# A Strassen cross-attention kernel: combinations summed in PSUM banks that are read in between, neighbouring groups of products interleaved, each engine's order written out

## Chip, cores and metric

One NeuronCore of a Trainium2 chip runs the whole program. The metric is the device time of one execution in microseconds (us), as a median of three runs. TensorE is PE in the profile, VectorE DVE, ScalarE ACT, GpSimd POOL; SP issues most DMAs.

## What is computed

For each of 32 batches, with C = 256 channels and N = 1024 positions, all in float32:

```python
x_q = jnp.einsum('oc,bcn->bno', w_qk, y)
x_k = jnp.einsum('oc,bcn->bon', w_qk, x)
x_v = jnp.einsum('oc,bcn->bon', w_v, x) + b_v[None, :, None]
energy = jnp.einsum('bnc,bcm->bnm', x_q, x_k)
attention = jax.nn.softmax(energy, axis=-1)
attention = attention / (1e-07 + attention.sum(axis=1, keepdims=True))
x_r = jnp.einsum('bcn,bnm->bcm', x_v, attention)
x_r = jax.nn.relu(jnp.einsum('oc,bcn->bon', w_t, x - x_r) + b_t[None, :, None])
return x + x_r
```

Here y is `ctx_2048`. The kernel folds the weights: energy is y against (w_qk^T w_qk) x, and w_t is multiplied into w_v once, at the start.

## The kernel before

Each large product of a batch is a 2x2 block product done with seven products instead of eight (Strassen in Winograd's form): products p1 to p7 of block sums, then sums of the products. There are four such groups in a batch:

- `keys` (L240): seven products of 128x512 from the folded weights and the blocks and sums of x (`xs`). They give `gx`, and four POOL sums of its blocks give `gt`.
- `values` (L278): seven products, each as four position tiles of 128 columns, so eight instructions (a float32 matmul is two instructions). They give `ut`, and four POOL sums `us`.
- `energy` (L366): for each of four tiles t, seven products of 128x512. DVE adds two parts into the rows `e` and takes their minimum or maximum in the same instruction (`block`, L384); ACT takes the exponential of the two rows of 1024 (L414); `share` (L427) adds the rows, divided by their sums, into `acc` (L433).
- `attend` (L461): after `columns` (L437) has formed rc, the inverse column sums, through one small product pS (L445), DVE multiplies the rows of e by both scales (`normal`, L471, rows of 1024) and forms four block sums (`less`, L477). Each of the seven products is one x-part (`xpart`, L489) and four tiles of e (`epart`, L494) in one bank. Results go through ACT (bias and Relu), POOL (adds x, L511) and SP (stores).

In `keys`, `values` and `attend` a first product p1 is copied out, p5 is copied out and p6 is summed onto p5's bank; every other product has a bank of its own. PSUM has eight banks, taken in turn by `bank` (L69). `kept` (L208) is the ACT copy out of a bank.

The loop over batches (L552) runs the four energy tiles of batch b, then keys and values of batch b + 1, then `columns` and `attend` of batch b. A scheduler of the tile framework orders the instructions of each engine; `tc.issue_after` pins a few POOL operations and the first product of an energy tile behind others. The sums of x and y blocks are formed by DMA: plain loads on SP's queue and three accumulating DMAs each on POOL's queue (`inputs` L214, `queries` L343, `accumulate` L98), `xsteps` during the energy tiles and `ysteps` after the keys.

Of the kernel before, what the change touches and what calls it, by code (L numbers as in the profile page):

```python
# [9 lines left out]
F32 = mybir.dt.float32  # L10
# [6 lines left out]
def kernel(  # L17
# [56 lines left out]
    def load_x(b, pieces=1):  # L74
        xt = xp.tile([P, KC, N], F32, tag="x", name=f"x_{b}")
        from_ = x[b].rearrange("(k p) n -> p k n", p=P)
        W = KC // pieces
        for j in range(pieces):
            nc.sync.dma_start(xt[:, ts(j, W)], from_[:, ts(j, W)])
        loaded[b] = xt  # L80

    def load_y(b):
        yt = yp.tile([P, KC, N], F32, tag="y", name=f"y_{b}")
        nc.sync.dma_start(yt, y[b].rearrange("(k p) n -> p k n", p=P))
        return yt
# [12 lines left out]
    def accumulate(into, from_):  # L98
        return nc.gpsimd.dma_start(into, from_, accum_op=ALU.add)
# [15 lines left out]
    uc = const.tile([P, 3, P], F32, name="uc")  # L115
    fold = const.tile([P, NG, G32], F32, name="fold")
    nc.sync.dma_start(wqk, w_qk.rearrange("(k p) c -> p k c", p=P))
    load_x(0, KC)
# [4 lines left out]
    yt = load_y(0)  # L123


    zeros = scratch[:, 5, :MB]
# [6 lines left out]
    def lefts(name, ps, sign=1.0):  # L133
# [13 lines left out]
        stt(s1, p21, -1.0, a22, ALU.add)  # L147
        stt(s3, p11, 1.0, a21, ALU.subtract)
        stt(s2, p11, -1.0, s1, ALU.subtract)
        stt(s4, p12, -1.0, s2, ALU.subtract)  # L150
# [26 lines left out]
    def value_bias(wtT):  # L177


        bvb = scratch[:, 6, : KC * P].rearrange("p (k c) -> p k c", k=KC)  # L180
        pb = bank("pb")
        for k in range(KC):
            nc.vector.tensor_copy(bvb[:, k, :], bv[:, k, :].to_broadcast([P, P]))
            nc.tensor.matmul(
                pb[:, :C], bvb[:, k, :], wtT[:, k, :], start=(k == 0), stop=(k == KC - 1)
            )
        nc.scalar.mul(uc[:, 0, :], pb[:, :P], -1.0)
        nc.vector.tensor_tensor(uc[:, 1, :], pb[:, P:C], uc[:, 0, :], ALU.add)
        nc.scalar.mul(uc[:, 2, :], pb[:, P:C], -2.0)
# [12 lines left out]
    def temp(tag, name, pool=cp):  # L202
        return pool.tile([P, MB], F32, tag=tag, name=name)

    def matmul(into, lhs, rhs, onto=False):
        nc.tensor.matmul(into, lhs, rhs, start=not onto, stop=True, skip_group_check=onto)  # L206

    def kept(p, tag, name, pool=cp):  # L208

        s = temp(tag, name, pool)  # L210
        nc.scalar.copy(s, p)  # L211
        return s

    def inputs(b):  # L214

        xs = up.tile([P, 4, MB], F32, tag="xs", name=f"xs_{b}")
        t1, t3, t4, t2 = (xs[:, j] for j in range(4))
        xq = quarters(x[b])
        if b == 0:
            xt = loaded[b]  # L220
            x11, x12 = xt[:, 0, ts(0, MB)], xt[:, 0, ts(1, MB)]
            x21, x22 = xt[:, 1, ts(0, MB)], xt[:, 1, ts(1, MB)]
            add(t1, x11, x12)
            add(t2, x22, t1)
            add(t3, x12, x22)
            add(t4, x21, t2)
            steps = []
        else:
            nc.sync.dma_start(xs[:, :2], xq[:, 0, 1:2, :].to_broadcast([P, 2, MB]))
            nc.sync.dma_start(xs[:, 2:], xq[:, 1])  # L230
            steps = [
                lambda: accumulate(xs[:, :2], corners(x[b])),
                lambda: accumulate(xs[:, 2:], xs[:, 0:1].to_broadcast([P, 2, MB])),
                lambda: accumulate(t4, xq[:, 1, 1]),
            ]
        return (lambda xt: (
            xt[:, 0, ts(0, MB)], xt[:, 1, ts(0, MB)], xt[:, 1, ts(1, MB)], t4, t1, t2, t3
        )), steps

    def keys(b, xr):  # L240

        gx = one.tile([P, KC, N], F32, tag="gx", name=f"gx_{b}")
        g11, g12 = gx[:, 0, ts(0, MB)], gx[:, 0, ts(1, MB)]
        g21, g22 = gx[:, 1, ts(0, MB)], gx[:, 1, ts(1, MB)]

        def gproduct(into, j, onto=False):
            matmul(into, g_left[j - 1], xr[j - 1], onto)

        p1, p2, p3, p4, p56, p7 = (bank(f"pg{j}_{b}") for j in (1, 2, 3, 4, 5, 7))
        gproduct(p1, 1)  # L250
        p1s = kept(p1, "p1s", f"g1s_{b}")
        gproduct(p2, 2)
        gproduct(p56, 5)
        p5s = kept(p56, "p5s", f"g5s_{b}")
        nc.vector.tensor_tensor(g11, p2, p1s, ALU.add)
        gproduct(p3, 3)
        gproduct(p7, 7)
        gproduct(p56, 6, onto=True)
        w = temp("w", f"gw_{b}")
        nc.vector.tensor_tensor(w, p56, p1s, ALU.add)  # L260
        nc.vector.scalar_tensor_tensor(g22, p7, -1.0, w, ALU.mult, ALU.subtract)
        nc.vector.scalar_tensor_tensor(g12, p3, -1.0, w, ALU.mult, ALU.subtract)
        v = temp("v", f"gv_{b}")
        if b == 0:
            nc.vector.tensor_tensor(v, g22, p5s, ALU.add)
        else:
            add(v, g22, p5s)
        gproduct(p4, 4)
        nc.vector.tensor_tensor(g21, p4, v, ALU.subtract)
        gt = one.tile([P, 4, MB], F32, tag="gt", name=f"gt_{b}")  # L270
        t1, t2, t3, t4 = (gt[:, j] for j in range(4))
        sub(t1, g12, g11)
        sub(t3, g22, g12)
        sub(t2, g22, t1)
        last = sub(t4, t2, g21)
        return (g11, g21, g22, t4, t1, t2, t3), last

    def values(b, xr):  # L278

        ut = up.tile([P, NT, C], F32, tag="ut", name=f"ut_{b}")  # L280

        def uproduct(into, j, onto=False):

            for t in range(HT):
                nc.tensor.matmul(  # L285
                    into[:, ts(t, P)],
                    xr[j - 1][:, ts(t, P)],
# [6 lines left out]
        def tiles(p):  # L294
            return p.rearrange("p (t c) -> p t c", t=HT)

        def bias(i):
            return uc[:, i : i + 1, :].to_broadcast([P, HT, P])

        def quadrant(half, i):  # L300
            return ut[:, half * HT : half * HT + HT, ts(i, P)]

        def block(half, i, p, s):
            nc.vector.tensor_tensor(quadrant(half, i), tiles(p), s, ALU.add)  # L304

        def biased(p, i, tag, name):

            s = temp(tag, name)
            nc.vector.tensor_tensor(tiles(s), tiles(p), bias(i), ALU.subtract)
            return s  # L310

        p1, p3, p4, p56, p7 = (bank(f"pu{j}_{b}") for j in (1, 3, 4, 5, 7))
        uproduct(p56, 5)
        p5s = biased(p56, 2, "p5s", f"u5s_{b}")
        uproduct(p1, 1)
        p1s = biased(p1, 0, "p1s", f"u1s_{b}")
        uproduct(p3, 3)
        uproduct(p7, 7)
        uproduct(p4, 4)
        uproduct(p56, 6, onto=True)  # L320
        w = temp("w", f"uw_{b}")
        nc.vector.tensor_tensor(w, p56, p1s, ALU.add)
        w1 = temp("v", f"uw1_{b}")
        add(tiles(w1), tiles(w), bias(1))
        block(1, 0, p3, tiles(w))
        uproduct(p1, 2, onto=True)
        block(0, 0, p1, bias(0))
        block(1, 1, p7, tiles(w1))
        v = temp("v", f"uv_{b}")
        last = sub(tiles(v), quadrant(1, 1), tiles(p5s))  # L330
        block(0, 1, p4, tiles(v))
        us = up.tile([P, 4, HT, P], F32, tag="us", name=f"us_{b}")
        s1, s2, s3, s4 = (us[:, j] for j in range(4))
        a11, a12, a21, a22 = quadrant(0, 0), quadrant(1, 0), quadrant(0, 1), quadrant(1, 1)
        steps = [
            lambda: add(s1, a21, a22),
            lambda: sub(s2, s1, a11),
            lambda: sub(s3, a11, a21),
            lambda: sub(s4, a12, s2),
        ]  # L340
        return (a11, a12, s4, a22, s1, s2, s3), steps, last

    def queries(b, yt):  # L343

        ys = one.tile([P, 4, MB], F32, tag="ys", name=f"ys_{b}")
        s3, s1, s2, s4 = (ys[:, j] for j in range(4))
        y11, y12 = yt[:, 0, ts(0, MB)], yt[:, 1, ts(0, MB)]
        y21, y22 = yt[:, 0, ts(1, MB)], yt[:, 1, ts(1, MB)]
        yq = quarters(y[b])
        if b == 0:  # L350
            add(s1, y21, y22)
            add(s2, s1, y11)
            add(s3, y11, y21)
            add(s4, y12, s2)
            steps = []
        else:
            nc.sync.dma_start(ys[:, :2], yq[:, 0, 1:2, :].to_broadcast([P, 2, MB]))
# [257 lines left out]
```

## Time and profile before

| | |
|---|---|
| median of 3 runs | 2506.15 us (2501.49 to 2508.46) |
| the profiled execution | 2508.91 us, of which its span 2507.0 us |
| TensorE busy | 2284.4 us, 91% of the span, 6366 matmuls |
| VectorE busy | 1821.6 us, 73% |
| ScalarE busy | 607.6 us, 24% |
| GpSimd busy | 1191.8 us, 48% |
| mean granted TensorE clock | 0.957 |

Matmuls are pipelined, so the records of neighbouring ones overlap: what a product costs is read from the distance between starts, not from the mean duration of a record. A stage of the work is read by windows of time, a wait by what ended it, and the chain of work by the timeline of one period.

### The profile page before, as it was taken

Reading aid. Unit: us, or ns where it says so; the run is one execution under the profiler, and the core shown is the slowest. Engines: PE = TensorE matmul, PEld = TensorE weight load, DVE = VectorE, ACT = ScalarE, POOL = GpSimd, SP = SyncE. Lnnn points to the kernel's source line nnn. Section 1 sums busy time; section 2 is a strip of 40 time slices with the busy share of each in tenths; the row PEclk is TensorE's granted clock in tenths of the full one; section 3 lists DMA queues with packets and bytes.
Section 4 is the critical chain, followed back from the end, with each engine's and each line's share of the span. In section 5 each row is a group of like instructions: output and inputs, shape, how many; then the busy total and the mean of one; then the engine's idle time right before and its main releaser. Section 6 shows DMA issues by size and latency. Waiting matters only on the chain.

```text
span 2507.0 us, 20193 instructions
## 1 busy us (share of the span) xinstructions
PE 2284.4 (91%) x6366; PEld 1096.3 (44%) x6366; DVE 1821.6 (73%) x3125; ACT 607.6 (24%) x1033; POOL 1191.8 (48%) x839
## 2 busy tenths in 40 slices
PE   9988899899999999999899988999888999899997
PEld 5444444444444444344444444444444434444442
DVE  6778767787677786777867768677787667876776
ACT  3212232122221222311223212232122321222212
POOL 5444544445544545444454444544445444455442
PEclk9999999999999999999999999999999999999998
DMA  4333443444344344434444333443344334443420
GB/s 134 89 102 88 116 110 88 109 92 110 105 104 99 96 101 113 118 82 101 91 121 110 87 99 88 122 110 88 109 88 112 107 88 109 96 106 105 103 61 17
DMA packets 109739, 249.05 MB, mean 99 GB/s; under 512 B 8640, under 2 KB 9408, under 8 KB 109632
## 3 DMA queue, kind: packets, MB, share of 16 engines
q0 software_dynamic: 42656, 81.28, 19.9%
q1 hardware_dynamic: 66432, 166.48, 19.8%
q8 instruction: 51, 0.84, 0.1%
q14 instruction: 56, 0.46, 0.1%
q10 hardware_dynamic: 544, 0.00, 0.0%
HBM read 181.67 MB, written 33.55 MB: 86 GB/s over the span
## 4 chain that ended last, share of the span: by engine, by line
PE 66%; DVE 16%; POOL 11%; issue 4%; DMA 3%; ACT 1%; POOLq 0%; ACTq 0%; DVEq 0%
PE po L496 32%; PE pe L206 24%; POOL v L64 4%; PE pg L206 4%; PE pu L285 3%; DVE e L473 3%; POOL gt L67 3%; DMA xs<-in_x_dram 3%; PE po L490 2%; DVE ut L304 2%; DVE acc L433 2%; DVE e L388 2%; DVE rc L456 1%; POOL gv L64 1%; POOL uw L64 1%
## 5 line engine op out<-in xcount | busy, mean ns | idle before, releaser
L511 POOL TENSOR_TENSOR ot<-ot,x 128x512 f32<-128x512 f32 x128 | 255.0, 1992 | 543.7 <-ACT ot L510 543.7
L64 POOL TENSOR_TENSOR v<-e,p5s 128x512 f32<-128x512 f32 x128 | 218.7, 1709 | 434.5 <-DVE nm L388 434.5
L206 PE MATMUL pe<-gt,ys 128*128 128x512 f32 x768 | 387.2, 601 | 0.6 <-ACT p5s L211 0.3
L496 PE MATMUL po<-e,ut 128*128 128x512 f32 x512 | 291.1, 707 | 103.9 <-DVE e L473 101.3
L473 DVE SCALAR_TENSOR_TENSOR e<-e,ri,rc 128x1024 f32<-128x1024 f32 x256 | 311.6, 1279 | 1.1
L433 DVE SCALAR_TENSOR_TENSOR acc<-e,ri,acc 128x1024 f32<-128x1024 f32 x224 | 290.9, 1299 | 1.2
L206 PE MATMUL pe<-gx,y 128*128 128x512 f32 x512 | 261.4, 592 | 0.0
L496 PE MATMUL po<-et,us 128*128 128x512 f32 x512 | 231.0, 594 | 1.1
L206 PEld LDWEIGHTS pe<-gt,ys 128*128 128x128 f32 x768 | 140.6, 190 | 205.5 <-issue 145.7
L496 PE MATMUL po<-e,us 128*128 128x512 f32 x512 | 230.2, 592 | 0.0
L496 PEld LDWEIGHTS po<-e,ut 128*128 128x128 f32 x512 | 107.5, 222 | 279.8 <-DVE e L473 193.1
L414 ACT ACTIVATE e<-e,nm 128x1024 f32<-128x1024 f32 x128 | 147.0, 1149 | 255.0 <-DVE nm L388 255.0
L414 ACT ACTIVATE e<-e,bias 128x1024 f32<-128x1024 f32 x128 | 147.0, 1149 | 234.3 <-DVE bias L411 234.3
L388 DVE CUSTOM_DVE_ANT_0 e<-pe,v,nm 128x512 f32<-128x512 f32 x128 | 96.1, 751 | 147.7 <-POOL v L64 147.7
L211 ACT COPY o1s<-po 128x512 f32<-128x512 f32 x32 | 18.8, 586 | 702.2 <-PE po L496 702.2
L496 PEld LDWEIGHTS po<-et,us 128*128 128x128 f32 x512 | 96.5, 190 | 129.3 <-issue 126.2
L496 PEld LDWEIGHTS po<-e,us 128*128 128x128 f32 x512 | 97.3, 190 | 122.5 <-issue 122.5
L480 DVE TENSOR_TENSOR et<-e,et 128x1024 f32<-128x1024 f32 x128 | 150.7, 1219 | 0.0
L206 PEld LDWEIGHTS pe<-gx,y 128*128 128x128 f32 x512 | 97.2, 190 | 122.0 <-issue 99.3
L206 PE MATMUL pe<-gt,y 128*128 128x512 f32 x256 | 130.7, 592 | 0.0
L206 PE MATMUL pe<-gx,ys 128*128 128x512 f32 x256 | 130.7, 592 | 0.0
L388 DVE CUSTOM_DVE_ANT_0 e<-pe,p1s 128x512 f32<-128x512 f32 x128 | 87.0, 680 | 59.6 <-PE pe L206 59.6
(123 smaller groups left out, 3596.1 us busy)
## 6 DMA issues: line engine op xcount, KB each, us to landing
y<-in_ctx_dram SPq DMA_DIRECT2D x32, 1024.0 KB, 8.8
out_dram<-ot SPq DMA_DIRECT2D x128, 256.0 KB, 2.0
x<-in_x_dram SPq DMA_DIRECT2D x31, 1024.0 KB, 5.8
xs<-in_x_dram SPq DMA_DIRECT2D x62, 512.0 KB, 4.2
ys<-in_ctx_dram SPq DMA_DIRECT2D x62, 512.0 KB, 6.7
xs<-in_x_dram POOLq DMA_DIRECT2D x31, 512.0 KB, 6.1
xs<-xs POOLq DMA_DIRECT2D x31, 512.0 KB, 5.0
ys<-in_ctx_dram POOLq DMA_DIRECT2D x31, 512.0 KB, 5.9
```

The costliest lines, as they stand in the source:

```text
L64: return nc.gpsimd.tensor_tensor(out_, in0, in1, ALU.add)
L67: return nc.gpsimd.tensor_tensor(out_, in0, in1, ALU.subtract)
L206: nc.tensor.matmul(into, lhs, rhs, start=not onto, stop=True, skip_group_check=onto)
L285: nc.tensor.matmul(into[:, ts(t, P)], xr[j - 1][:, ts(t, P)], u_left[j - 1], start=(t == 0 and not onto), stop=(t == HT - 1), skip_group_c ...
L304: nc.vector.tensor_tensor(quadrant(half, i), tiles(p), s, ALU.add)
L388: nc.vector.tensor_tensor_reduce(out=e[:, n, ts(h, MB)], in0=in0, in1=in1, scale=1.0, scalar=(BIG if n < HT else -BIG) if first is None el ...
L414: nc.scalar.activation(e[:, n, :], e[:, n, :], AF.Exp, bias=bias[n], scale=-1.0 if n == low else 1.0, accum_out=rs,)
L433: nc.vector.scalar_tensor_tensor(acc, e[:, n, :], scales[n], acc, ALU.mult, ALU.add)
L473: nc.vector.scalar_tensor_tensor(e[:, n, :], e[:, n, :], scales[n], rc, ALU.mult, ALU.mult)
L480: nc.vector.tensor_tensor(out_[:, two], in0[:, two], in1[:, two], ALU.subtract)
L496: last = nc.tensor.matmul(into[:, cols], ur[j - 1][:, t], er[j - 1][:, t, cols], start=False, stop=(t == HT - 1), skip_group_check=True,)
L511: nc.gpsimd.tensor_tensor(ot, ot, xt[:, i, there], ALU.add)
```

## The change

The four groups become subclasses of one class `Seven`. A group now has three banks: `one` takes p1, then p6, p7 and p4 summed onto it; `two` takes p5, then p3; `three` takes p2. Between these, the running sum is read out of the bank: after p1 (p1s), after p5 (p5s), after p6 (w), after p7 (c22), after p4 (c21). Each read is one that the next product onto the bank has to wait for.

- An `InOrder` wrapper fixes the order of instructions on TensorE, VectorE, ScalarE and GpSimd to that of the text. DMAs issued by `nc.sync` are not in it.
- p4 of an energy tile comes in the next tile, behind p6; that of the last tile among the keys; the attention's p4 (`end`) behind p5 of the next batch's first energy tile.
- Keys, values and the end of the energy are interleaved; parts of the values (u.c22, u.p4, u.c21, u.c11, u.c12) lie inside `Attention.run`.
- `normal` works on halves of rows (512 columns). The first share is done by ACT (`acc` = scaled copy).
- The last energy block is the bank itself plus a tile of zeros (DVE); POOL's v sums go. The energy's operands change sides (y's sums are the stationary ones).
- The attention's bias is added by ACT when it copies p1s, p5s and w (Identity with bias); DVE does max(z, 0) + x in one operation. POOL's output add goes.
- The values' bias is added by an accumulating DMA from a broadcast row (`bias`). `us` has one buffer, not two. The loads of x are one batch later in the text.

The diff, cut to its core:

```diff
+    class InOrder:
+        def __getattr__(self, name):
+            def call(*args, **kwargs):
+                behind = nullcontext() if self.last is None else tc.issue_after(self.last.ins)
+                with behind:
+                    self.last = getattr(self.engine, name)(*args, **kwargs)
+                return self.last
...
+    pe, dve, act, pool = (InOrder(g) for g in (nc.tensor, nc.vector, nc.scalar, nc.gpsimd))
...
+        def p1(self):
+            self.one = self.bank(1)
+            self.product(self.one, 1)
+            self.p1s = self.kept(self.one, "p1s")
+
+        def p5(self):
+            self.two = self.bank(5)
+            self.product(self.two, 5)
+            self.p5s = self.kept(self.two, "p5s")
+
+        def p2(self):
+            self.three = self.bank(2)
+            self.product(self.three, 2)
+
+        def p6(self):
+            self.product(self.one, 6, True)
+            self.w = self.kept(self.one, "w")
+
+        def p3(self):
+            self.product(self.two, 3, True)
+
+        def p7(self):
+            self.product(self.one, 7, True)
+
+        def p4(self):
+            self.product(self.one, 4, True)
+
+        def c11(self):
+            self.combine(0, 0, self.three, self.p1s, ALU.add)
+
+        def c12(self):
+            self.combine(0, 1, self.two, self.w, ALU.subtract)
+
+        def c22(self):
+            self.combine(1, 1, self.p5s, self.one, ALU.subtract)
...
+            pool.tensor_tensor(s1, a21, a22, ALU.subtract)
+            pool.tensor_tensor(s2, s1, a11, ALU.subtract)
+            pool.tensor_tensor(s3, a11, a21, ALU.subtract)
+            pool.tensor_tensor(s4, s2, a12, ALU.add)
...
+        def bias(self):
+            accumulate(self.ut, uc.to_broadcast([P, NT, C]))
...
+        def c21(self):
+            self.combine(1, 0, self.one, zeros, ALU.add)
...
+        def biased(self, p, tag, bias):
+            s = temp(tag, f"o{tag}_{self.b}")
+            act.activation(s, p, AF.Identity, bias=bias, scale=1.0)
+            return s
...
+        def run(self, u):
+
+            self.normal(0, 0)
+            if u:
+                u.c22()
+            self.normal(1, 0)
+            self.normal(0, 1)
+            self.mix(self.t1, self.b11, self.b12, ALU.add)
+            self.normal(1, 1)
+            self.mix(self.t2, self.t1, self.b22, ALU.subtract)
+            self.epart(self.one, 1)
+            self.p1s = self.biased(self.one, "p1s", bt[:, 0, :])
+            if u:
+                u.p4()
+                u.c21()
+            self.epart(self.three, 2)
+            self.xpart(self.one, 6, True)
+            self.epart(self.two, 5)
+            self.p5s = self.biased(self.two, "p5s", bt[:, 1, :])
+            self.c11()
+            if u:
+                u.c11()
+                u.c12()
+            self.xpart(self.two, 3, True)
+            self.epart(self.two, 3, range(HT // 2))
+            self.epart(self.one, 6)
+            self.w = self.biased(self.one, "w", nbt[:, 0, :])
+            self.mix(self.t3, self.b12, self.b22, ALU.subtract)
+            self.mix(self.t4, self.b21, self.t2, ALU.subtract)
+            self.epart(self.two, 3, range(HT // 2, HT))
+            self.c12()
+            self.xpart(self.one, 7, True)
+            self.epart(self.one, 7)
+            self.c22()
...
+        for t in range(HT):
+            now = Energy(b, t, lhs, rhs)
+            pair.append(now)
+            now.p1()
+            if t > 0:
+                pair[t - 1].exp(1)
+            now.p5()
+            if t == 0:
+                if before is not None:
+                    before.end()
...
+            if t > 1:
+                pair[t - 2].share(0)
+            now.p2()
+            now.c11()
+            if t == 0 and before is not None:
+                before.c21()
+                if b + 1 < B:
+                    load("x", b + 1)
...
+            now.p6()
+            if t == 1:
+                act.activation(acc, e[:, HT, :], AF.Copy, scale=scales[HT])
+            if t > 0:
+                pair[t - 1].p4()
+                pair[t - 1].c21()
+                pair[t - 1].exp(0)
+            now.p3()
+            now.c12()
+            now.p7()
+            now.c22()
+            usteps[t]()
+            if more and t == 0:
+                xn, xsteps = summed("x", b + 1)
+            elif more:
+                xsteps[t - 1]()
...
+            g = Keys(b + 1, xn)
+            g.p1()
+        last.exp(1)
         if more:
+            g.p5()
+        pair[2].share(0)
+        last.p4()
+        last.c21()
+        last.share(1)
+        if more:
+            load("y", b + 1)
+            rhs, ysteps = summed("y", b + 1)
+            g.p6()
+        last.exp(0)
+        if more:
+            g.p2()
+            g.c11()
+            g.p3()
+        last.share(0)
+        part = columns(b)
+        if more:
+            g.p7()
+            g.c12()
+            g.c22()
+            un = Values(b + 1, xn)
+            un.p1()
+            un.p5()
+            un.p2()
+            un.p6()
+        rc = inverse(b, part)
+        if more:
+            un.p3()
+            g.p4()
+            g.c21()
+            un.p7()
+            lhs = g.factors()
+
+        now = Attention(b, xr, ur)
+        now.begin()
+        if more:
+            ysteps[0]()
+            now.run(un)
+            ysteps[1]()
+            un.bias()
+            ysteps[2]()
```

## Rows read from the trace of the kernel before

**Rows 1.** Windows by stage: length; busy PE, PEld, DVE, ACT, POOL; clock; DMA share; GB/s.

```profile
1185.40:1209.90 24.50, 24.49 (x57) 10.47 (x56) 16.54 (x41) 10.86 (x19) 12.18 (x11) 1.00 0.47 108
1209.90:1221.70 11.80, 7.44 (x15) 2.85 (x14) 10.54 (x24) 4.68 (x8) 5.97 (x5) 0.89 0.67 201
1221.70:1231.10 9.40, 9.40 (x61) 8.91 (x60) 4.85 (x8) 0.00 (x0) 7.51 (x7) 0.77 0.21 32
1231.10:1264.00 32.90, 30.59 (x70) 12.59 (x69) 24.97 (x26) 3.30 (x5) 12.33 (x8) 1.00 0.33 79
```

**Rows 2.** TensorE's waits: line, releaser, us in total, times, longest.

```profile
PE po L496 <- DVE e L473: 101.3, 31, 4.9
PE pg L206 <- DMA xs<-in_x_dram: 46.3, 20, 3.3
PE pg L206 <- ACT g5s L211: 24.0, 31, 0.8
```

**Rows 3.** Timeline of TensorE in the attention: start, us, operation, idle before.

```profile
1245.89 3.60 PE L496 MATMUL po<-e,ut 128*128 128x512 f32 x8
1249.32 3.60 PE L496 MATMUL po<-e,us 128*128 128x512 f32 x8
```

**Rows 4.** Timeline of TensorE in keys and values.

```profile
1215.18 1.13 PE L206 MATMUL pg<-xs,gs 128*128 128x512 f32 x2 [0.78 <-ACT g5s L211]
1219.88 2.05 PE L206 MATMUL pg<-xs,g 128*128 128x512 f32 x2 [3.58 <-DVE gx L261]
...
1228.24 1.06 PE L285 MATMUL pu<-wvtTs,xs 128*128 128x128 f32 x8
1229.13 1.06 PE L285 MATMUL pu<-wvtT,x 128*128 128x128 f32 x8
```

**Rows 5.** Timeline of TensorE: first and last batch's first energy product, pS, last product.

```profile
24.84 1.02 PE L206 MATMUL pe<-gx,y 128*128 128x512 f32 x2
...
2430.35 1.02 PE L206 MATMUL pe<-gx,y 128*128 128x512 f32 x2
...
2465.86 0.63 PE L445 MATMUL pS<-part,fold 128*128 128x32 f32 x2 [10.81 <-DVE ri L454]
...
2495.75 3.60 PE L496 MATMUL po<-et,ut 128*128 128x512 f32 x8
```

**Rows 6.** Groups of instructions by form: shapes, count, busy us, mean ns, idle before.

```profile
L433 DVE SCALAR_TENSOR_TENSOR acc<-e,ri,acc 128x1024 f32<-128x1024 f32 x224 | 290.9, 1299 | 1.2
L414 ACT ACTIVATE e<-e,nm 128x1024 f32<-128x1024 f32 x128 | 147.0, 1149 | 255.0 <-DVE nm L388 255.0
L388 DVE CUSTOM_DVE_ANT_0 e<-pe,v,nm 128x512 f32<-128x512 f32 x128 | 96.1, 751 | 147.7 <-POOL v L64 147.7
L510 ACT ACTIVATE ot<-c,bt 128x512 f32<-128x512 f32 x64 | 46.2, 722 | 337.1 <-DVE c L530 273.9 <-DVE c L534 63.2
L211 ACT COPY g5s<-pg 128x512 f32<-128x512 f32 x32 | 18.8, 587 | 1.1 <-PE pg L206 1.1
```

**Rows 7.** Timeline of VectorE around rc and in the block sums.

```profile
1232.24 0.35 DVE L450 RECIPROCAL sc<-sc 128x32 f32<-128x32 f32 x1
...
1234.10 1.24 DVE L456 STREAM_TRANSPOSE rc<-sc 128x1024 f32<-128x1024 f32 x1
...
1251.76 2.35 DVE L480 TENSOR_TENSOR et<-e,et 128x1024 f32<-128x1024 f32 x2
```

**Rows 8.** Timeline of GpSimd at the end of the attention.

```profile
1250.29 4.94 POOL L511 TENSOR_TENSOR ot<-ot,x 128x512 f32<-128x512 f32 x1 [10.66 <-ACT ot L510]
...
1261.52 1.27 POOL L67 TENSOR_TENSOR ov<-c,o5s 128x512 f32<-128x512 f32 x1 [0.69 <-DVE c L534]
```

**Rows 9.** DMA issues: destination and source, queue, count, KB each, median us to landing.

```profile
xs<-in_x_dram POOLq DMA_DIRECT2D x31, 512.0 KB, 6.1
xs<-xs POOLq DMA_DIRECT2D x31, 512.0 KB, 5.0
...
xs<-in_x_dram POOLq DMA_DIRECT2D x31, 256.0 KB, 8.5
```

More of the change, by code (lines that the diff above doesn't have):

```diff
@@ L200, with temp @@
     sp = ctx.enter_context(tc.tile_pool(name="sp", bufs=4))
-    def temp(tag, name, pool=cp):
-        return pool.tile([P, MB], F32, tag=tag, name=name)
+    def temp(tag, name):
+        return cp.tile([P, MB], F32, tag=tag, name=name)
     def matmul(into, lhs, rhs, onto=False):
[L206 to L218, printed above, removed]
-        if b == 0:
[L220 to L226, printed above, removed]
+        pe.matmul(into, lhs, rhs, start=not onto, stop=True, skip_group_check=onto)
@@ L236, in inputs @@
[L236 to L276, printed above, removed]
@@ L292, in uproduct, with tiles @@
                 )
-        def tiles(p):
+        def tiles(self, p):
             return p.rearrange("p (t c) -> p t c", t=HT)
[L297 to L357, printed above, removed]
-            nc.sync.dma_start(ys[:, 2:], yq[:, :, 0])
+        def block(self, i, h):
+            return self.ut[:, h * HT : h * HT + HT, ts(i, P)]
@@ L359, in queries @@
             steps = [
[L360 to L391 removed]
+                lambda: pool.tensor_tensor(s1, a21, a22, ALU.add),
@@ L478, in less @@
             for j in range(HT // 2):
                 two = ts(j, 2)
[L480 to L499 removed]
+                dve.tensor_tensor(out_[:, two], in0[:, two], in1[:, two], op)
@@ L500, in epart, with xpart @@
+        def xpart(self, into, j, onto=False):
+            pe.matmul(
+                into, t_left[j - 1], self.xr[j - 1], start=not onto, stop=False, skip_group_check=True
+            )
+        def epart(self, into, j, tiles=range(HT)):
+            for t in tiles:
+                pe.matmul(
+                    into,
+                    self.ur[j - 1][:, t],
+                    self.er[j - 1][:, t],
                     start=False,
@@ L552 @@
+    u.c12()
+    u.p7()
+    u.c22()
+    u.p4()
+    u.c21()
+    u.bias()
+    before = None
     for b in range(B):
         more = b + 1 < B
-        e = ep.tile([P, NT, N], F32, tag="e", name=f"e_{b}")
-        acc = one.tile([P, N], F32, tag="acc", name=f"acc_{b}")
-        if more:
-            sums, xsteps = inputs(b + 1)
-        for t in range(HT):
-            with tc.issue_after(last.ins) if (t == 0 and b > 0) else nullcontext():
-                behind = energy(b, t, lhs, rhs, e)
-            for step in usteps[t : t + 1] + (xsteps[t : t + 1] if more else []):
-                with tc.issue_after(behind.ins):
-                    behind = step()
-            if t > 0:
-                share(e, acc, t - 1)
@@ L567 @@
-        share(e, acc, HT - 1)
-        if more:
-            xn = sums(loaded[b + 1])
-            yt = load_y(b + 1)
-            lhs, ysteps = queries(b + 1, yt)
-            rhs, behind = keys(b + 1, xn)
-            with tc.issue_after(behind.ins):
-                ysteps[0]()
-            un, usteps, behind = values(b + 1, xn)
-            for step in ysteps[1:]:
-                with tc.issue_after(behind.ins):
-                    behind = step()
-        rc = columns(b, acc)
-        last = attend(b, xr, ur, e, rc)
@@ new lines @@
+        if more:
+            g.p7()
+            g.c12()
+            g.c22()
+            un = Values(b + 1, xn)
[6 more added lines that the diff above has]
+            un.p3()
+            g.p4()
+            g.c21()
+            un.p7()
+            lhs = g.factors()
+        now = Attention(b, xr, ur)
[6 more added lines that the diff above has]
+            ysteps[2]()
+            before = now
+            xr, u = xn, un
+        else:
+            now.run(None)
+            now.end()
+            now.c21()
```

390 lines of the change are left out of this document (203 added, 187 removed).

## The prediction

> **What bounds the kernel now.** I read the stages first. One period, from the first energy product of a batch to that of the next, is 78.6 us in the slice shown, and TensorE (PE) is busy in nearly all of the energy stage but in only 7.44 of the 11.8 us of the keys stage; no other engine is near its limit, for VectorE (DVE) sums to 56.9 us over the four stages [rows 1]. The list of TensorE's waits says which wait ends last: normalised attention rows (101.3 us), x sums that arrive late by DMA (46.3 us), and a ScalarE (ACT) copy of a product that must be read before the next product may go onto its bank, 31 times 0.8 us [rows 2].
>
> The unit of the sum is one product of two 128x512 instructions. Eight instructions begin at 1245.89 and the next eight at 1249.32, so a product takes 3.43/4 = 0.858 us [rows 3]. A values product (eight instructions of 128 columns) takes 1229.13 - 1228.24 = 0.89 us [rows 4]. A batch has 28 energy, 7 key and 35 attention products (7 x-parts, 7 of four tiles) and 7 value products: 70 x 0.858 + 7 x 0.89 = 66.3, with pS (two instructions of 32 columns, at most two of the eight above, so under 0.22; I take 0.2) **66.5 us**. Thirty-one periods lie between 24.84 and 2430.35 [rows 5]: 77.6 us each. So 11.1 us of a period are waits or half clock, and that is all the change can win, since it removes no product. In the slice: keys 11.8 against 7 x 0.858 = 6.0; values with one x-part 9.4 against 7.3; attention with the other 34 products 32.9 against 29.2; energy 24.5 against 24.0. The loss in the values is clock: the granted clock there is 0.77, with gaps of 0.78 and 3.58 us ahead of it in the keys [rows 1, 4].
>
> **The change, part by part.** *Products interleaved.* Keys now wait between their own products. In the new order g.p6, p2, p3, p7 (3.43 us) and un.p1, p5, p2, p6 (3.57) run while DVE and ACT finish the last energy tile; pS, un.p3, g.p4, un.p7 and three x-parts (0.2 + 0.89 + 0.86 + 0.89 + 2.57 = 5.4) run while DVE forms rc. So epart(1) can start 12.4 us after the end of the last energy p4 (time 0). DVE, at their durations [rows 6, 7]: c21 to 0.75, share(1) to 2.05; exp(0) on ACT starts after g.p6 and its copy (0.86 + 0.59) and ends at 2.6; g.c11 meanwhile, share(0) with its reciprocal to about 4.1; columns (taken as the transpose of the same shape, 1.24) 5.4, so pS at 7.0 has its input; g.c12, g.c22 to 6.9; after pS two small operations of at most 0.35 and the transpose, 7.2 + 0.7 + 1.24 = 9.1. Normalising is cut into halves of 512 columns: half of share's 1.30, 0.65 each (no such form is shown; below, 0.61 by the pitch that back-to-back operations would keep; above, 0.75 of the energy block; I take 0.65, the same operation at half the columns). The first tile is ready at 9.75, 2.6 us ahead of its use; before, four whole rows stood ahead of the first e-part. The 101.3 us go, and what is late next is checked along the same chain: t1's first half is ready at 9.1 + 12 x 0.65 + 0.75 + 1.2 = 18.9 (a pair of such sums takes 2.35 [rows 7]), and epart(5) needs it at 12.4 + 3.43 + 0.89 + 3.43 + 0.86 = 21.0. t3, at about 30, is needed at 34. The least slack is 2.1 us.
>
> *Banks used twice.* Each group of seven now has three banks and four hand-offs, where a product waits until ACT or DVE has read the bank; TensorE's later products are queued behind each. One uncovered hand-off to ACT is the row with 0.78 us of idle [rows 4] (a copy of 0.587 [rows 6] and 0.2 of signals); to DVE it is 0.75 + 0.2 = 0.95. Cover: p1 to p6, two products (1.7 us); p6 to p7, one or more (0.86 at least); p7 to p4, two products where it is least; p5 to p3, two or three. One has none: in the attention xpart 3 follows epart(5) at once. Its reader is an Identity with bias, which is not shown: between the copy's 0.587 and the biased Relu's 0.722; I take the second, as it also adds a bias. So + 0.9 us a period. Within an energy tile, ACT does p1's copy, exp of the tile before, p5's copy: 0.9 + 0.6, to 2.75, to 3.4, and p3 is due at 4.3. If that cover is gone, each tile pays up to 0.8.
>
> *DVE's and POOL's work.* Off DVE: four w sums of energy, two operations in keys and four in values (10 x about 0.7) and the first share, now ACT's; on it: three more in the attention. That is some 6 us less of 56.9, so about 51 in the new period: not the bound, but an exact order makes each lateness queue. GpSimd (POOL) loses the output add and the energy v sum; this work was mostly hidden, and I count no gain for it beyond the chain above. ACT gains seven w copies, two c21 copies and the acc scaling (9 x 0.59 + 1.15), loses three Relus (2.2): some 4 us in an engine that is mostly idle.
>
> *DMA.* New: the bias of the values as an accumulating transfer of 1 MB a batch in POOL's queue, behind ysteps[1] and ahead of ysteps[2] and of the next batch's usteps and xsteps. Price: xs<-xs moves 512 KB in 5.0 us [rows 9]; twice the bytes give 10, four times the pieces (1 KB each, not 2) give 20. I take 12, nearer to the bytes. Issued at about 34, it lands at 46; the first us sum then runs at 47 to 50, before the x loads are in, and nothing on the path waits. At 20 it delays the x sums (rival 2). The xs loads may start only when the last x-part of the attention before has read the tile, which now lies in the next energy stage (about 40; 46 if SP keeps the order of the text behind the x load). With 6 us to load, then 7, 6 and 7 us for three accumulations [rows 9], t2 is there at 59 to 65 and needed at 67.
>
> **The sum.** Period: 66.5 + 0.9 + 0.4 for waits that I can't place (the energy stage already loses 24.5 - 24.0) = **67.8 us**. Before the first energy product: 24.84 now, plus one uncovered DVE hand-off (u.p4 on u.p7's bank), 25.7. Last batch: nothing covers it. 63 products x 0.858 = 54.1; p4 behind c22 0.95; from p4 to pS c21, two shares with exp(0) and columns, 5.0 (10.81 idle before [rows 5]); pS 0.2; three x-parts at half clock + 2.6; p5s 0.9; xpart 4 behind c22 0.95; and a tail, now 2507.0 - 2495.75 - 3.43 = 7.8 [rows 5], without POOL's add 6.5. Together 71.2. Total 25.7 + 31 x 67.8 + 71.2 = 2198.7 us of span, + 1.9 (the profiled run's 2508.9 against its span of 2507.0) = 2200.6; the profiled run lies 2.8 above the median of 2506.15, so I forecast **2200**. At the floor of 66.5 a period it is 2160.
>
> **Rivals.** *1, POOL starved.* An output add issued at 1250.29 took 4.94 us where another took 1.27, and ended 1.1 us after the back-to-back DVE sums that end at 1254.11: POOL waited for DVE's whole run [rows 7, 8]. The new order puts g.factors (four POOL adds) where DVE normalises and sums with hardly a pause from 9 to 32 us, and ysteps[0] is queued behind them. s1 to s3 can start at 6.9, when DVE works on PSUM and small tiles; only s4 needs g.c21 (9.6). If the adds first get through when DVE rests at about 33, ysteps[0] lands at 34 + 6.1 = 40 and p5 of the next energy, due at 38.2, waits 2 to 3 us: 70.5 a period, **2284**. Against it: DVE's reads of banks between 24 and 27 leave room. The Trainium skill, SBUF — State Buffer, Who interferes with whom, says that a DVE instruction with two SBUF inputs keeps out a GpSimd instruction that reads SBUF; the trace agrees by its 4.94 us, and by that rule this rival holds wherever no one-input operation falls in between.
>
> *2, x sums late.* With the bias at 20 us, usteps end at 57 and t2 comes at 57 + 7 + 6 = 70, 3 us late: 70.8, **2293**. For it: 46.3 us of this wait already [rows 2], and a transfer's landing of up to 8.5 us for 256 KB [rows 9]. That SP's queue is not among the orders fixed by hand belongs here: the change then does only part of what it says.
>
> *3, clock.* If a gap of about a microsecond a period lowered the clock, the products behind it would run at half rate as in the values stage now (2.1 us lost, and part of the keys): + 2.7, **2284**. Against it: after the 0.78 us gap the pair of products took 1.13 us, and the attention stage shows a granted clock of 1.00 [rows 1, 4]. The Trainium skill, TensorE: Matmul & The Clock Gate, A second HAM failure mode, reports a kernel whose cycling through PSUM banks idled TensorE often enough to make its clock fall again and again; no run here shows that yet.
>
> *4, slower.* Hand-offs uncovered in general: each order is fixed, so if ACT or DVE lags TensorE by one product, all 28 hand-offs of a period stop it. 28 x 0.78 = 21.8 us make 88.3 a period and **2830**; more than 14 of the 28 uncovered (11 / 0.78) decide for slower. Against it: covers of 0.86 to 4 us at all but one.
>
> **Chances.** Forecast (2160 to 2240) 0.60; rival 1 0.10; rival 2 0.12; rival 3 0.06; a few hand-offs uncovered (2310 to 2490) 0.05; equal 0.03; rival 4 0.04. The range from the floor to a period of 71.3, 2162 to 2310, holds the forecast and rivals 1 to 3. Faster than by 0.3% (about what a measurement of this kernel can tell from no change) 0.93, within it 0.03, slower 0.04.
>
> **What would show it.** Right: periods of 67 to 69 us, a granted clock near 1.00 in every stage, TensorE's waits led by xpart 3 behind ACT with 0.9 us each, none on normalised rows. Wrong: a wait of TensorE on ys (rival 1) or xs (rival 2), a clock below 0.95 without long gaps (3), or waits on ACT copies and DVE combinations spread over energy tiles (4). The forecast fails most easily at the DMA chains, where the trace before shows least.

## The result and the profile after

The changed kernel takes **2219.47 us** (2216.27 to 2220.56), 0.886 of the kernel before (95% interval 0.8841 to 0.8884); 2200 was forecast, in a range of 2162 to 2310. Its profiled execution took 2216.27 us with a span of 2214.5 us. Line numbers no longer tell operations apart, since all go through the wrapper at L77; the names of the tiles do (`op5s` is the attention's copy of p5, `et` its block sums t1, t2, t4, `ep1s` and `ew` the energy's copies).

The page's line of busy time, share of the span and instructions:

```profile
PE 2166.1 (98%) x6366; PEld 1054.7 (48%) x6366; DVE 1772.2 (80%) x2963; ACT 785.2 (35%) x1321; POOL 617.5 (28%) x488
```

TensorE's waits (us in total, times, longest), the three longest:

```profile
PE po L77 <- ACT op5s L77: 26.8, 32, 0.8
PE po L77 <- DVE et L77: 5.4, 21, 0.3
PE pS L77 <- DVE part L77: 5.3, 1, 5.3
```

Windows of one period: keys with the last energy p4; values with pS, g.p4 and three x-parts; attention; the next energy tiles with the attention's p4.

```profile
core 0: us, PE busy (x) PEld busy (x) DVE busy (x) ACT busy (x) POOL busy (x), PEclk, DMA share, GB/s
1004.59:1010.85 6.26, 6.26 (x16) 2.58 (x14) 5.97 (x16) 5.14 (x9) 0.00 (x0) 1.00 0.90 283
1010.85:1019.87 9.02, 9.02 (x60) 7.11 (x59) 8.61 (x10) 2.35 (x4) 5.21 (x4) 1.00 0.10 38
1019.87:1045.56 25.69, 24.57 (x64) 10.99 (x63) 23.29 (x29) 2.65 (x4) 5.54 (x5) 1.00 0.51 85
1045.56:1073.78 28.22, 27.82 (x66) 11.93 (x65) 18.31 (x40) 14.21 (x24) 8.45 (x7) 1.00 0.69 165
```

The same 6366 matmuls run; the granted clock is 1.00 in all four stages, where the values had 0.77 [rows 1]. All three waits of [rows 2] are gone: rows and xs are in no wait of TensorE any more, and g5s is covered. The first window's seven products (six of the keys and the last energy p4) take 6.26 us, where the seven of the keys took 11.8 before; pure product time is 6.0. What is left stands in the attention, 25.69 us for six e-parts of four tiles, three x-parts and u.p4, 27 x 0.858 + 0.89 = 24.1. (The energy window is 0.8 us above its 32 products, most of it a ScalarE copy, ep1s, that came late here and one other time in the run.) The timeline shows where the attention's time goes:

```profile
1019.87 3.60 PE L77 MATMUL po<-e,ut 128*128 128x512 f32 x8
1023.30 1.05 PE L77 MATMUL pu<-wvtT,xs 128*128 128x128 f32 x8
1024.19 3.60 PE L77 MATMUL po<-e,ut 128*128 128x512 f32 x8
1027.63 1.02 PE L77 MATMUL po<-xs,wtTs 128*128 128x512 f32 x2
1028.93 3.67 PE L77 MATMUL po<-et,us 128*128 128x512 f32 x8 [0.28 <-DVE et L77]
1033.44 1.12 PE L77 MATMUL po<-x,wtTs 128*128 128x512 f32 x2 [0.84 <-ACT op5s L77]
1034.40 1.88 PE L77 MATMUL po<-e,us 128*128 128x512 f32 x4
```

epart(5) begins 1028.93 - 1027.63 - 0.86 = 0.44 us late; xpart 3 begins 1033.44 - 1028.93 - 3.43 = 1.08 us late, of which 0.84 is recorded as idle, and the next product comes another 0.10 late (0.96 for 0.86). A short gap costs some 0.2 to 0.3 us beyond the idle that the record shows: 0.16 because a product's record (1.02 us) outlasts the distance between starts (0.86), and about 0.1 because the product behind the gap takes longer.

Why t1 is late: VectorE's timeline in the same period,

```profile
1016.66 5.09 DVE L77 SCALAR_TENSOR_TENSOR e<-e,ri,rc 128x512 f32<-128x512 f32 x4
1021.67 0.67 DVE L77 TENSOR_TENSOR ut<-up5s,pu 128x512 f32<-128x512 f32 x1
1022.27 5.38 DVE L77 SCALAR_TENSOR_TENSOR e<-e,ri,rc 128x512 f32<-128x512 f32 x8
```

and GpSimd's:

```profile
1017.15 1.72 POOL L77 TENSOR_TENSOR gt<-gx 128x512 f32<-128x512 f32 x1
1018.83 1.71 POOL L77 TENSOR_TENSOR gt<-gt,gx 128x512 f32<-128x512 f32 x1
```

The four half rows that run beside g.factors take 5.09 us, the next eight 5.38: 1.27 against 0.67 each, so VectorE loses 2.4 us there. The second and third half row by themselves (VectorE's timeline):

```profile
1017.66 1.75 DVE L77 SCALAR_TENSOR_TENSOR e<-e,ri,rc 128x512 f32<-128x512 f32 x1
1019.34 1.75 DVE L77 SCALAR_TENSOR_TENSOR e<-e,ri,rc 128x512 f32<-128x512 f32 x1
```

Each ends some 0.55 us behind the end of one of GpSimd's adds (19.41 behind 18.87, 21.09 behind 20.54): the two engines take turns.

The ends of the run: the first batch's first energy product, the last batch's, and pS of the last batch.

```profile
24.90 1.02 PE L77 MATMUL pe<-gx,y 128*128 128x512 f32 x2
...
2139.96 1.02 PE L77 MATMUL pe<-gx,y 128*128 128x512 f32 x2
...
2175.10 0.63 PE L77 MATMUL pS<-part,fold 128*128 128x32 f32 x2 [5.25 <-DVE part L77]
```

The p4 of an attention (five 512-column products, 4.3 us) now lies in the next period, which the first period lacks: a full period is (2139.96 - 24.90 + 4.3)/31 = 68.37 us, against 67.8 in the sum and 77.6 before [rows 5].

### The profile page after: what moved, and what is told of

Same layout as the page of the kernel before. It is cut to its first block, busy times and chain, and to the rows that moved or that the text cites. A ratio compares the mean times of both kernels' runs of the same rounds, so it can differ in the third digit from the quotient of the medians.

```text
span 2214.5 us, 19880 instructions
## 1 busy us (share of the span) xinstructions
PE 2166.1 (98%) x6366; PEld 1054.7 (48%) x6366; DVE 1772.2 (80%) x2963; ACT 785.2 (35%) x1321; POOL 617.5 (28%) x488
## 4 chain that ended last, share of the span: by engine, by line
PE 81%; DVE 16%; ACT 2%; issue 1%; ACTq 0%; DVEq 0%
PE po L77 34%; PE pe L77 32%; DVE e L77 11%; PE pg L77 7%; PE pu L77 7%; DVE rc L77 1%; DVE et L77 1%; ACT op5s L77 1%; DVE acc L77 1%; DVE ut L77 1%; DVE sc L77 1%; ACT e L77 0%; PE pS L77 0%; PE idle L142 0%; ACT ep1s L77 0%
## 5 line engine op out<-in xcount | busy, mean ns | idle before, releaser
L77 DVE SCALAR_TENSOR_TENSOR e<-e,ri,rc 128x512 f32<-128x512 f32 x512 | 416.9, 878 | 1.1
L77 PE MATMUL pe<-gt,ys 128*128 128x512 f32 x768 | 395.4, 596 | 0.7 <-ACT ep1s L77 0.7
L77 DVE SCALAR_TENSOR_TENSOR acc<-e,ri,acc 128x1024 f32<-128x1024 f32 x224 | 309.5, 1381 | 8.0
L77 DVE CUSTOM_DVE_ANT_0 e<-pe,ep1s 128x512 f32<-128x512 f32 x128 | 88.3, 690 | 240.3 <-PE pe L77 176.4
L77 PE MATMUL pe<-gx,y 128*128 128x512 f32 x512 | 261.5, 592 | 0.0
L77 PE MATMUL po<-et,us 128*128 128x512 f32 x512 | 232.5, 597 | 5.7 <-DVE et L77 5.4
L77 PE MATMUL po<-e,us 128*128 128x512 f32 x512 | 235.4, 592 | 0.0
L77 PEld LDWEIGHTS pe<-gt,ys 128*128 128x128 f32 x768 | 142.7, 190 | 191.4 <-issue 157.3
L77 PE MATMUL po<-e,ut 128*128 128x512 f32 x512 | 230.1, 592 | 0.0
L77 POOL TENSOR_TENSOR gt<-gx 128x512 f32<-128x512 f32 x64 | 94.8, 1481 | 412.6 <-DVE gx L77 412.6
L77 ACT ACTIVATE e<-e,nm 128x1024 f32<-128x1024 f32 x128 | 147.1, 1149 | 127.3 <-DVE nm L77 125.9
L77 ACT COPY ep1s<-pe 128x512 f32<-128x512 f32 x128 | 74.5, 582 | 274.0 <-PE pe L77 273.6
L77 PEld LDWEIGHTS po<-et,us 128*128 128x128 f32 x512 | 94.7, 190 | 138.1 <-issue 123.0
L77 POOL TENSOR_TENSOR us<-ut 128x512 f32<-128x512 f32 x64 | 95.9, 1499 | 229.3 <-PE pe L77 155.9
L77 PEld LDWEIGHTS po<-e,us 128*128 128x128 f32 x512 | 97.3, 190 | 122.5 <-issue 108.1
L77 PEld LDWEIGHTS pe<-gx,y 128*128 128x128 f32 x512 | 97.2, 190 | 122.0 <-issue 121.5
L77 ACT ACTIVATE e<-e,bias 128x1024 f32<-128x1024 f32 x128 | 147.3, 1151 | 1.1 <-DVE ri L77 0.5
L77 PEld LDWEIGHTS po<-e,ut 128*128 128x128 f32 x512 | 94.9, 190 | 107.6 <-issue 79.2
L77 POOL DMA_DIRECT2D ut<-uc x32 | 50.7, 1584 | 312.6 <-DVE ut L77 298.7
L77 PE MATMUL pe<-gx,ys 128*128 128x512 f32 x256 | 132.3, 598 | 1.9 <-DVE nm L77 1.0
L77 PE MATMUL pe<-gt,y 128*128 128x512 f32 x256 | 130.7, 592 | 0.0
L77 POOL DMA_DIRECT2D xs<-in_x_dram x62 | 65.8, 1062 | 192.3 <-PE pe L77 96.3
```

The lines of the kernel that those rows point to most:

```text
L77: self.last = getattr(self.engine, name)(*args, **kwargs)
```

## Experiments

The changed kernel again and the first three variants ran on one chip, the others on two more, each beside the kernel before (2505, 2508 and 2509 us on the three). A difference between chips is therefore good to some 4 us.

**The changed kernel again**, 2219.4 us, 0.8855 (0.8831 to 0.8880).

> The changed kernel itself, run beside the variants on one chip so that differences of less than one per cent can be read. Every theory: 0.886 of the kernel before, periods of 68.3 us, of which 66.5 us of products.

**Sums of the keys later.** The four POOL sums move behind the bias and the last y sum in POOL's queue:

```diff
             un.p7()
-            lhs = g.factors()
...
             ysteps[2]()
+            lhs = g.factors()
```

> The four POOL sums of the keys (g.factors) are issued behind ysteps[2] instead of ahead of ysteps[0], so they no longer run while VectorE normalises. Theory A (POOL's sums hold up VectorE: the first four normalised half rows take 5.09 us where the next eight take 5.38): the first four take 2.7 us, all later VectorE work comes 2.4 us earlier, TensorE's waits on t1 (et, 5.4 us in all, and as much again in late starts) vanish, the period falls by 0.3 to 0.45 us: 10 to 14 us, 0.880 of the kernel before. Theory B (the half rows are slow by their form, mean 0.88 us): the mean stays at 0.88 and the time stays. Rival 1 of the prediction (POOL starved) expects a gain from the earlier ysteps[0] only if TensorE waited on ys, which it did not: no gain.

2206.7 us, 0.8809 (0.8785 to 0.8833): 12.7 us less. VectorE's timeline at the first four half rows:

```profile
1011.91 2.74 DVE L77 SCALAR_TENSOR_TENSOR e<-e,ri,rc 128x512 f32<-128x512 f32 x4
```

The group of all half rows (busy us, mean ns), whose mean was 878 ns:

```profile
L77 DVE SCALAR_TENSOR_TENSOR e<-e,ri,rc 128x512 f32<-128x512 f32 x512 | 347.3, 746 | 1.1
```

2.74 for 5.09, and the wait on et is no longer in the list. Theory A held in size; theory B (slow by form) fell.

**Two products behind epart(5).**

```diff
-            if u:
-                u.p4()
-                u.c21()
             self.epart(self.three, 2)
-            self.xpart(self.one, 6, True)
             self.epart(self.two, 5)
             self.p5s = self.biased(self.two, "p5s", bt[:, 1, :])
+            if u:
+                u.p4()
+                u.c21()
+            self.xpart(self.one, 6, True)
```

> u.p4, u.c21's copy and xpart 6 are moved behind epart(5), between it and xpart 3: 0.89 + 0.86 = 1.75 us of products for the hand-off that had none. Theory A: the wait on op5s (26.8 us in all, 0.84 a period) vanishes with its late restart (about 0.2), but epart(5) begins 1.75 us earlier and t1 is already late by 0.3: its wait grows to about 2 us, so the period rises by 0.5 to 0.9 us (15 to 30 us slower, 0.895 of the kernel before). Theory C (the hand-off alone sets the period, t1 has slack as the prediction worked it out): 1.0 us a period gained, 32 us, 0.873.

2234.95 us, 0.892 (0.8895 to 0.8945): 15.6 us slower than the changed kernel, as theory A had it. op5s has left the list of waits; its first line is now:

```profile
PE po L77 <- DVE et L77: 56.0, 31, 2.0
```

The gap ahead of epart(5) is 1.75 to 1.92 us in 26 of the 31 periods and about 2.0 in five. Behind four of those five TensorE ran some products at half rate (the clock's level of 1.2 GHz), behind none of the others. One of each, in TensorE's timeline:

```profile
72.98 5.37 PE L77 MATMUL po<-et,us 128*128 128x512 f32 x8 [1.99 <-DVE et L77]
...
1038.56 3.67 PE L77 MATMUL po<-et,us 128*128 128x512 f32 x8 [1.75 <-DVE et L77]
```

The granted clock is 0.72 from 72 to 78 us.

**Both together.**

> Both of the two: sums of the keys late, and the two products behind epart(5). Theory A: t1 is ready 2.4 us earlier and the hand-off is covered: both waits vanish, periods of 66.7 to 66.9 us, 1.4 to 1.7 us a period less than the changed kernel, 43 to 52 us, 0.866 of the kernel before. Theory B: as the second run alone, since VectorE gains nothing. Theory C: 0.873, no more than the second run.

2170.47 us, 0.866 (0.8636 to 0.8684): 48.9 us less than the changed kernel, the fastest of all. One edit gains 12.7, the other loses 15.6, both gain 48.9: the two products that cover the hand-off behind epart(5) stood in front of it before and gave t1 time there. With t1 late, moving them turns a wait of 0.28 us into one of 1.75; with t1 earlier by 2.4 us they are free to move. TensorE's attention now runs without a break (starts 3.43, 0.89 and 0.86 apart):

```profile
1007.35 3.60 PE L77 MATMUL po<-et,us 128*128 128x512 f32 x8
1010.78 1.05 PE L77 MATMUL pu<-wvtT,xs 128*128 128x128 f32 x8
1011.67 1.02 PE L77 MATMUL po<-xs,wtTs 128*128 128x512 f32 x2
1012.53 1.02 PE L77 MATMUL po<-x,wtTs 128*128 128x512 f32 x2
```

**Whole rows** (on the sums-later kernel): was it the cutting of rows into halves that took the 101 us of waits away?

```diff
-                cols = e[:, n, ts(h, MB)]
+                cols = e[:, n, :]
                 dve.scalar_tensor_tensor(
-                    cols, cols, scales[n], rc[:, ts(h, MB)], ALU.mult, ALU.mult
+                    cols, cols, scales[n], rc, ALU.mult, ALU.mult
                 )
...
-            self.normal(0, 0)
+            self.normal(0)
...
-            self.normal(1, 0)
-            self.normal(0, 1)
+            self.normal(1)
             self.mix(self.t1, self.b11, self.b12, ALU.add)
-            self.normal(1, 1)
```

> Built on e1_late. Rows are normalised whole (1024 columns, eight instructions of about 1.2 us pitch, instead of sixteen halves of 0.67), the lower rows ahead of t1 as before. Theory A (the products laid over the chain from the last energy p4 to rc took the 101 us of waits away; halves only add slack): first rows are ready at 1.3, 2.5, 3.7, 4.9 us after rc, the first e-part begins 3.2 us after rc and needs its tiles at 3.2, 4.1, 4.9, 5.8: no wait; epart(2) up to 0.3 us: 0 to 12 us slower than e1_late, 0.881 to 0.886 of the kernel before. Theory E (cutting the rows into halves took the waits away): two to three us a period come back, 60 to 100 us slower than e1_late, 0.905 to 0.92.

2217.06 us, 0.8838 (0.8817 to 0.8858), 10 us more than with halves (7 by the ratios to the kernel before, since the chips differ). No wait on rows stands in TensorE's list; in its timeline epart(2) takes 0.3 us longer, as worked out:

```profile
1025.73 3.90 PE L77 MATMUL po<-e,ut 128*128 128x512 f32 x8
```

So the halves give 7 to 10 us; the 101 us of waits on rows [rows 2] don't come back without them.

**Less cover** (on the sums-later kernel): the last energy tile's p4 5.2 us later in TensorE's order.

```diff
         pair[2].share(0)
-        last.p4()
-        last.c21()
         last.share(1)
         if more:
-            load("y", b + 1)
-            rhs, ysteps = summed("y", b + 1)
             g.p6()
-        last.exp(0)
-        if more:
             g.p2()
             g.c11()
             g.p3()
...
             un.p1()
             un.p5()
+        last.p4()
+        last.c21()
+        last.exp(0)
...
```

> Built on e1_late. The last energy tile's p4 moves behind four key products and two value products (5.2 us later in TensorE's order), with all that follows from it (its block, exp(0), the last share, the column sums). Cover between it and pS falls from 7.0 to 1.8 us, while c21, exp(0), share(0) and columns need about 4.7: TensorE waits 2.9 us at pS and starts late by another 0.2, 3.1 us a period, 96 us slower than e1_late, 0.919 of the kernel before. The same products, only the place of one changed. Rival 3 of the prediction (a gap lowers the clock): the products after this gap run at half rate for some us, 2 to 3 us more a period, 160 to 190 us slower, 0.945 to 0.957. Theory E (halves, not cover): under 20 us slower.

2431.28 us, 0.9698 (0.9679 to 0.9717): 224.6 us slower, more than any theory had. TensorE's timeline, pS and the products behind it:

```profile
1042.95 0.41 PE L77 MATMUL pS<-part,fold 128*128 128x32 f32 x2 [5.00 <-DVE part L77]
1043.19 2.02 PE L77 MATMUL pu<-wvtTs,x 128*128 128x128 f32 x8
1045.00 1.85 PE L77 MATMUL pg<-xs,g 128*128 128x512 f32 x2
1046.69 1.05 PE L77 MATMUL pu<-wvtTs,xs 128*128 128x128 f32 x8
```

VectorE's timeline ahead of it:

```profile
1036.27 0.69 DVE L77 TENSOR_TENSOR gx<-pg,gp1s 128x512 f32<-128x512 f32 x1 [3.85 <-PE pe L77]
1036.87 0.68 DVE L77 TENSOR_TENSOR gx<-pg,gw 128x512 f32<-128x512 f32 x1
1037.47 0.68 DVE L77 TENSOR_TENSOR gx<-gp5s,pg 128x512 f32<-128x512 f32 x1
1038.07 0.74 DVE L77 CUSTOM_DVE_ANT_0 e<-pe,zeros,nm 128x512 f32<-128x512 f32 x1
```

The wait is 5.0 us, not 2.9: gx has one buffer, the late p4 still reads the old one, so g.c11 waited for it, and three combinations (1.8 us) ran ahead of c21. Two products behind the gap are then 1.81 and 1.69 us apart instead of 0.89 and 0.86: half rate again, and so it is behind this gap in all 31 periods.

**Less cover, g.c11 to g.c22 behind c21.** Against the run above, this puts that cause to the test.

```diff
             g.p2()
-            g.c11()
             g.p3()
             g.p7()
-            g.c12()
-            g.c22()
...
         last.c21()
         last.exp(0)
...
+            g.c11()
         last.share(0)
         part = columns(b)
...
+            g.c12()
+            g.c22()
```

> As e5_cover (the last energy p4 5.2 us later in TensorE's order), but VectorE's g.c11, g.c12 and g.c22 stand behind the block c21 and not ahead of it. In e5_cover g.c11 waited for that p4 (3.85 us of idle on VectorE, ended by TensorE) and the three, 1.8 us, ran ahead of c21, which made the wait at pS 5.0 us instead of 2.9. Theory A with that cause: the wait at pS falls by 1.8 to 2.0, to about 3.1 us a period; whether the clock falls behind a gap of 3.1 us as it did behind 5.0 (0.88 over the 14.2 us that follow p4) is open: with it 4.9 us a period, 150 us slower than e1_late, 0.941 of the kernel before; without it 3.3, 100 us, 0.921. If the 5.0 us had another cause (the clock or a transfer), the wait stays at 5 us and the time at 0.970.

2364.97 us, 0.9421 (0.9393 to 0.9450), 158 us slower than the sums-later kernel. In TensorE's list of waits the one at pS fell, as that cause has it:

```profile
PE pS L77 <- DVE part L77: 104.1, 32, 6.7
```

Without the last batch's 6.7 it is 3.14 us a period, where the run above has 5.0. The same gap of 3.14 us was followed by full rate in 15 periods and by half rate in 16; here one of each in TensorE's timeline, from pS on:

```profile
1014.61 0.41 PE L77 MATMUL pS<-part,fold 128*128 128x32 f32 x2 [3.14 <-DVE part L77]
1014.85 1.14 PE L77 MATMUL pu<-wvtTs,x 128*128 128x128 f32 x8
1015.83 1.08 PE L77 MATMUL pg<-xs,g 128*128 128x512 f32 x2
...
1157.31 0.63 PE L77 MATMUL pS<-part,fold 128*128 128x32 f32 x2 [3.14 <-DVE part L77]
1157.76 2.05 PE L77 MATMUL pu<-wvtTs,x 128*128 128x128 f32 x8
1159.61 1.91 PE L77 MATMUL pg<-xs,g 128*128 128x512 f32 x2
```

The granted clock is 1.00 and 0.77 in windows around the two. From pS to the next pS it is 71.35 us behind the first and 74.42 behind the second, where the sums-later kernel has 68.0 in most periods: the gap costs 3.3 us, half rate behind it another 3.1.

**One more hand-off exposed per energy tile** (on the fastest kernel):

```diff
             now.p6()
+            now.p7()
...
             now.c12()
-            now.p7()
             now.c22()
```

> Built on e3_latefill. In every energy tile p7 comes at once behind p6 on the same bank, ahead of the other tile's p4 and of p3, so that the copy w stands uncovered: 128 of the 896 hand-offs. Theory A (rival 4's price, 0.78 to 0.84 of idle and 0.2 of late restart each): 128 x 1.0 = 125 to 140 us slower than e3_latefill, 0.916 to 0.922 of the kernel before. If short gaps lower TensorE's clock (rival 3): the energy stage loses clock as well, beyond 0.95. If PSUM hand-offs cost nothing by themselves (the engines' lag matters, not the place): under 30 us.

2292.77 us, 0.9143 (0.9125 to 0.9160): 122.3 us more than the kernel that it is built on, 0.96 us for each of the 128. TensorE's list of waits:

```profile
PE pe L77 <- ACT ew L77: 90.5, 128, 1.1
```

0.71 of idle and 0.25 of late restart each; a little under the 125 to 140 expected. The mean granted clock stays at 0.998 with a gap in every energy tile.

**Orders left to the scheduler.**

```diff
-                behind = nullcontext() if self.last is None else tc.issue_after(self.last.ins)
+                behind = nullcontext()
```

> The changed kernel with the four engines' orders left to the scheduler (the wrapper pins nothing); the text and all operations are the same. Theory A (where the products stand in the text gives the gain; pinning only keeps it): within 2% of the changed kernel, 0.88 to 0.905 of the kernel before. Theory F (the pinned order itself is the gain): the scheduler brings waits on rows and banks back, 0.93 to 1.0.

2224.66 us, 0.8873 (0.8855 to 0.8892), the same as pinned within the intervals, but by another way: op5s is not among the waits, because the scheduler moved part of epart(6) between epart(5) and xpart 3, and TensorE waits on et instead (its timeline):

```profile
1032.39 3.67 PE L77 MATMUL po<-et,us 128*128 128x512 f32 x8 [0.48 <-DVE et L77]
1037.31 1.10 PE L77 MATMUL po<-et,us 128*128 128x512 f32 x2 [1.25 <-DVE et L77]
1038.24 1.02 PE L77 MATMUL po<-x,wtTs 128*128 128x512 f32 x2
```

Pinning the orders by hand is no part of this kernel's gain: the same text without it takes the same time.

**No bias transfer in the loop.**

> The changed kernel without the accumulating DMA of the values' bias inside the loop (batches after the first lack that bias). Rival 2 of the prediction (the 1 MB transfer delays the x sums, on which TensorE then waits) expects a gain of up to 3 us a period, 0.85 to 0.88. Theory A (the transfer lands in 9.5 us, nothing on the path waits for it): within 0.3% of the changed kernel, 0.884 to 0.888.

2216.13 us, 0.8827 (0.8804 to 0.8850): 3 us below the changed kernel and a little under the 0.884 expected, but the intervals of both overlap; op5s waits as before (26.8 us), et a little less (3.2). Rival 2's gain of up to 3 us a period isn't there.

## Why the prediction was right, and where it was off

- **What bounds, and what can be won.** The unit of 0.858 us and the floor of 66.5 us a period held: the fastest kernel's 2170 lies 10 us above the 2160 that the prediction gives for the floor. The chain of work that ended last is now 81% TensorE.
- **Interleaving as the main term.** Right, and shown for the stretch from the last energy p4 to pS by taking cover away: with p4 5.2 us later 158 to 225 us are lost of the some 300 that the sums-later kernel had gained; of the 158, 31 x 3.3 = 103 are the gap and the rest the clock behind it. Halves of rows: the slack, worth 7 to 10 us. Not shown singly: what ended the waits among the keys' own products, and which part of the change ended the 46.3 us of waits on xs [rows 2], since no run gives back the old order of the loads alone.
- **Hand-offs.** Right in place, and nearly in size. One has no cover, xpart 3 behind p5s: 0.84 of idle and about 0.2 late, 1.0 to 1.1 us, where the sum had 0.9. The other exposed ones (u.p4 at the start, p4 and xpart 4 in the last batch) were put at 0.95 each; the idle recorded is 0.8 at u.p4 and at xpart 4 and 1.0 at p4.
- **The step that was mis-sized: slack of t1 and what POOL does there.** The prediction had t1 2.1 us ahead of its use. 2.4 us went to g.factors, which it treated as a rival with the wrong victim: it expected POOL to be kept out (as [rows 8] show) and ys to come late, whereas the adds and the half rows took turns, each held up by the other, and TensorE never waited on ys. So 2.1 us of slack became 0.3 of lateness: 0.28 of idle is recorded in the slice, and epart(5) began 0.44 late. Moving the sums gave 12.7 us back, 0.41 a period. A period has 68.37 - 66.5 - 0.9 = 0.97 us beyond the terms that the sum names, where it allowed 0.4: t1's 0.41, the 0.2 of the hand-off above, and some 0.35 of late starts of a tenth each (in the slice at the last energy p4, the key product behind it and the first tile's p7: 0.14, 0.11 and 0.08). So 0.57 a period, 31 x 0.57 = 17.7 us, were missing, and t1 is the larger part of it.
- **The edges.** 24.90 to the first energy product (25.7 forecast); 2214.5 - 2139.96 - 4.3 = 70.2 for the last batch (71.2), its wait at pS 5.25 (5.0). Together 1.8 us less than the sum. 2198.7 + 17.7 - 1.8 = 2214.6, the span. (24.84 + 0.95 is 25.8 where the prediction has 25.7, and 2200.6 - 2.8 is 2197.8 where it says 2200; neither matters.)
- **DMA.** The bias transfer was priced at 12 us and took 9.5; no wait on xs or ys stands in the list. Rival 2 fell, by the profile and by the run without the transfer. The page's DMA issues (KB each, median us to landing):

```profile
ut<-uc POOLq DMA_DIRECT2D x32, 1024.0 KB, 9.5
...
xs<-in_x_dram POOLq DMA_DIRECT2D x31, 512.0 KB, 9.1
```

- **Clock.** Rival 3 fell for gaps of this size: 128 gaps of 0.7 us left the clock at 0.998. The failure mode that the Trainium skill reports (TensorE: Matmul & The Clock Gate, A second HAM failure mode) did not appear with bank hand-offs alone. Behind longer gaps the clock did fall: behind none of the 26 of 1.75 to 1.92 us, four of the five of 2.0, 16 of the 31 of 3.14 and all 31 of 5.0.
- **Slower (rival 4).** Its price per hand-off, 0.78, was a little low: 0.96 in the run with 128 more of them, 0.71 of idle and 0.25 of late restart. Its condition, lag on all of them, did not arise.

## What to carry to other kernels

Price a product's order by hand-offs: each place where an engine must read a bank before the next product may use it costs about 1 us here when nothing lies between, and a tenth of that (0.08 us at the first energy tile's p7) when one product does and the reader is in time. When two waits stand in a row, the products that would cover one may be those that cover the other now, and moving them can make the kernel slower: look for what is late next and move both. An operation off the path (four GpSimd sums) can eat the slack of one on it, so look at what runs beside the tightest stretch of the chain, not only at what is in it.

## What the runs showed of the hardware beyond that

- GpSimd's adds and VectorE's operations with two inputs in SBUF held each other up in turns (half rows of 0.74 us took up to 1.75, adds of 1.27 took 1.72), where in the kernel before one add had waited through a whole run of VectorE sums (4.94 us [rows 8]). The Trainium skill (SBUF — State Buffer, Who interferes with whom) says that the order of issue decides who blocks; the trace agrees that either side can be the one that waits. What makes the two take turns in the one case and not in the other stays open.
- The same gap of 3.14 us on TensorE was followed by full rate in 15 periods and by half rate, for three products in the one shown, in 16. Over the runs the share grows with the gap (from none at 1.75 us to all at 5.0), but why one length goes both ways stays open.
- A short gap costs TensorE 0.2 to 0.3 us more than the idle recorded.
